# A fused graph layer and mixture of experts: VectorE's additions to node sums written one step behind their products, and a page's addition two steps behind

## The chip, the cores and the metric

The kernel runs on one core of one Trainium2 chip. Its engines are TensorE (PE: matrix products; PEld is its loading of weights), VectorE (DVE), ScalarE (ACT), GpSimd (POOL) and SyncE (SP). Each works through its own instruction stream in order; data passes between them through SBUF and, for products, through PSUM. The metric is the device time of one execution in microseconds (us).

## The reference, cut to what matters

There are 12,500 nodes with 256 features, and 212,500 weighted edges, sorted by destination. First a graph layer, then a mixture of experts with one expert a token:

```python
x = x + (segment_sum(layernorm(x)[src] * edge_weight[:, None], dst, 12500) @ W.T + b)
h = layernorm(x)                                     # tokens = nodes
probs = softmax(h @ gate_w + gate_b); idx = argmax(probs)      # 8 experts
# each expert takes at most C = 1954 tokens, in order
y = relu(h @ w1[idx] + b1[idx]) @ w2[idx] + b2[idx]            # 256 -> 1024 -> 256
x = x + nan_to_num(y * prob * kept)
```

The reference gathers a token over the limit from the last place of its expert and multiplies it by zero.

## The kernel before, in words

**Edges.** The 212,500 edges are cut into blocks of 128. For each block POOL gathers 128 rows of normalised features by an indirect DMA (`gather`, L708, into `m`). DVE builds a 128x128 mask `h` of destinations, scaled by edge weights (`onehot`, L731; L729 for self edges), and PE adds `h`-transposed times `m` into a sum `pw` of a group of 15 blocks, 1,920 edges (`product`, L742). When a group is done, ACT copies `pw` to SBUF as `ws` (L745; nine buffers). In the middle 88 groups, each group has 14 blocks of its own, and four groups share one further gather: 57 gathers for 4 groups. The blocks before round 112 are gathered from the raw input while a table of normalised features is written to HBM.

**The main loop.** After the table, everything is written by one Python loop with a counter (a *step* or *round* here). The order of instructions in each engine's stream is the order in which this loop writes them. In each round it writes, in this order: one gather (while there are any; the last is that of round 1594); an `own` load on SP at fixed rounds (L723); one of the `moves` (below; none in a round after a page's loads); one `put` of `pool_q` if there is one, or else one call of the generator that finishes the oldest computed page (`outs`); up to 8 masks ahead of need (`AHEAD`); one or two products, 16 gathers behind (`LEAD`); one call of each of a few start-up generators; one call of `nodes`; and one call of `experts`. A gather may not run more than 20 gathers ahead of the products (`LEASH`). A `yield` in a generator therefore means: what follows is written one round later.

**`nodes`** goes over the 98 tiles of 128 nodes, in chunks of 8 (the last chunks have 5, 4 and 1). For a tile it yields until the last group sum that the tile needs is there, and once more; writes the products that shift the group sums onto the tile (`pa`, L778), half by half with a yield after each; writes ACT's copy `aT` (L782) and the next tile's shift masks, and yields; writes two products with the weight matrix into `px` (L787), and then DVE's additions of `px` and the bias to the node's input, and its statistics (L790 and after). In PSUM, `pa`, `px` and other small products share the two buffers named `ms`. After a chunk comes `route`: gate, softmax, arg max and places; for the first ten chunks `sort` orders the chunk's tokens by expert and 64 `moves` (8 tiles x 8 experts) copy them to pages, one a round; for later chunks `put` scatters them through POOL. Then `listing` writes which pages of 128 tokens are full. `nodes` waits until the moves or puts have been written, and hands the listed pages on:

```python
                        while moves or pool_q:
                            yield
```

Up to chunk 9 pages are listed in pairs (33 pairs); from chunk 10 on singly (25 pages, of which the last 8 are the partly filled ones). `SLOTS` holds how many a chunk lists: (2, 4) for most, (1, 10) for chunk 10, then (1, 4) and (1, 3).

**`experts`** takes the pages one after another. SP loads a page and its expert's weights (L558 to L571, three buffers for weights and biases), up to two pages ahead; a page is started no sooner than 20 rounds after its loads (`LOADED`). Its product is a generator (`products`), called at paced rounds:

```python
PACE = {1: 2.3, 2: 3.0}
...
                    elif work and now[0] >= at:
                        at += PACE[got[0]]
```

The first layer is written in `ph` (L604) with ACT's relu into `hT` (L608), the second in `py` (L615; one buffer). Before a page's second layer, the next page is transposed (`turn`, L589). A single page takes its start and four calls, so 12 rounds; a pair takes its start and eight, 27 rounds.

**`finish`** ends a page, one part a call: DVE adds the bias to `py` (L625); ACT scales by the probability (L628); DVE clears non-finite values and adds the residual (L632 to L643, the last writes the row numbers `tok`); after three empty calls POOL scatters the rows to the output (L647, a *send*, one a call).

Of the kernel before, what the change touches and what calls it, by code (L numbers as in the profile page):

```python
# [122 lines left out]
def groups_of(t):  # L123
    return range(max(0, (P * PER * t - MARGIN) // GE),
                 min(NGR - 1, (P * PER * (t + 1) + MARGIN - 1) // GE) + 1)
# [12 lines left out]
def gnn_moe_kernel(ctx: ExitStack, tc: tile.TileContext, x, src, dst, ew, wT, gb, gate_w, gate_b,  # L138
# [85 lines left out]
    def ln_new(pool, n=CH):  # L224
        return pool.tile([P, n, 6], F32, name="bn"), pool.tile([P, n, 2], F32, name="mv")

    def ln_stats(ln, x_, j, rows):
        nc.vector.bn_stats(ln[0][:rows, j, :], x_)
        nc.vector.bn_aggr(ln[1][:rows, j, :], ln[0][:rows, j, :])
# [37 lines left out]
    class Ffn:  # L267
# [353 lines left out]
        def finish(self, of, pg, py, b2_sb):  # L621
            p4 = self.p4
            y = p4.tile([P, 2, D], F32, name="y", bufs=1)
            yv = y[:, :of, :]
            nc.vector.tensor_add(yv, py[:, :of, :], b2_sb[:, None, :].to_broadcast([P, of, D]))  # L625
            yield 1
            for a in range(of):
                nc.scalar.activation(y[:, a, :], y[:, a, :], AF.Copy, scale=pg[:, a, D + 2:D + 3])  # L628
            yield 1

            fin = p4.tile([P, 2, D], U8, name="fin")
            nc.vector.tensor_scalar(fin[:, :of, :], yv, 0.0, 0.0, op0=ALU.mult, op1=ALU.is_equal)  # L632
            hi = p4.tile([P, 2, D], F32, name="hi", bufs=1)
            nc.vector.tensor_scalar(hi[:, :of, :], yv, FLT_MAX, 1e4, op0=ALU.is_gt, op1=ALU.mult)
            z = p4.tile([P, 2, D], F32, name="z")
            zv = z[:, :of, :]
            nc.vector.tensor_scalar(zv, yv, -FLT_MAX, -1e4, op0=ALU.is_lt, op1=ALU.mult)
            yield 1
            nc.vector.tensor_add(zv, zv, hi[:, :of, :])
            nc.vector.copy_predicated(zv, fin[:, :of, :], yv)  # L640
            nc.vector.tensor_add(zv, zv, pg[:, :of, :D])
            to = p4.tile([P, 2, 1], I32, name="tok")
            nc.vector.tensor_copy(to[:, :of, :], pg[:, :of, D + 3:RW])  # L643

            def send(a):
                nc.gpsimd.nop()
                s = nc.gpsimd.indirect_dma_start(  # L647
                    out=out[:, :], out_offset=bass.IndirectOffsetOnAxis(ap=to[:, a, :], axis=0),
                    in_=z[:, a, :], in_offset=None, bounds_check=N - 1, oob_is_err=False)
                for o in self.sends:  # L650
                    tc.declare_no_dep(s.ins, o.ins, reason="each token is in one page")
                self.sends.append(s)

            for _ in range(3):
                yield 1
            for a in range(of):
                send(a)
                yield 1
# [20 lines left out]
    with tc.tile_pool(name="edges", bufs=1) as edges:  # L679
# [10 lines left out]
        with tc.tile_pool(name="p2", bufs=32) as p2, tc.tile_pool(name="p2h", bufs=12) as p2h, \  # L690
# [57 lines left out]
            def nodes():  # L748
                xs, shifts = [], {}

                def shift(t):

                    for g in groups_of(t) if t < NT else ():
                        s = p2o.tile([P, P], F32, name="s", bufs=8)
                        nc.vector.tensor_scalar(s, cols, float(P * t), win[:, g:g + 1], op0=ALU.add,
                                                op1=ALU.is_equal)
                        shifts[t, g] = s

                for c, (t0, nt, rows) in enumerate(CHUNKS):
                    rt = p3.tile([P, CH, RW], F32, name="rt")  # L760
                    ln = ln_new(p3)
                    for t in range(t0, t0 + nt):
                        for i in range(len(xs), min(t + 3, NT)):
                            x_ = p3.tile([P, D], F32, name="xt", bufs=4)
                            r = min(P, N - i * P)
                            nc.scalar.dma_start(x_[:r, :], x[i * P:i * P + r, :])
                            xs.append(x_)
                        if t == 0:
                            shift(t)
                        gs = groups_of(t)  # L770
                        while gs[-1] not in sums:
                            yield
                        yield
                        pa = ffn.psum("pa")[:, :2 * P]
                        aT = p2o.tile([P, 2 * P], F32, name="aT")
                        for k in range(2):
                            for g in gs:
                                nc.tensor.matmul(pa[:, k * P:(k + 1) * P],  # L778
                                                 sums[g][:, k * P:(k + 1) * P], shifts[t, g],
                                                 start=(g == gs[0]), stop=(g == gs[-1]))  # L780
                            yield
                        nc.scalar.copy(aT, pa)  # L782
                        shift(t + 1)
                        yield
                        px = ffn.psum("px")[:, :D]
                        for k in range(2):
                            nc.tensor.matmul(px[:rows, :], aT[:, k * P:k * P + rows], wT_sb[:, k, :],  # L787
                                             start=(k == 0), stop=(k == 1))
                        x1 = rt[:rows, t - t0, :D]
                        nc.vector.tensor_add(x1, xs[t][:rows, :], px[:rows, :])  # L790
                        nc.vector.tensor_add(x1, x1, gb_sb[:rows, :])
                        ln_stats(ln, x1, t - t0, rows)
                    yield from ffn.route(rt, ln, t0, nt, rows,
                                         by_expert[c % 3] if c < SORTED else None)
                    (moves if c < SORTED else pool_q).extend(ffn.put)
                    last = c == len(CHUNKS) - 1
                    if last:
                        nc.vector.scalar_tensor_tensor(n_bad, most, float(RUN), bad, op0=ALU.is_gt,
                                                       op1=ALU.add)
                    if last or SLOTS[c][1]:  # L800
                        if last:
                            lp = ffn.last()
                        yield from ffn.listing(*SLOTS[c] if not last else (1, LEFT, True))
                        li = ffn.li
                        while moves or pool_q:
                            yield
                        if last:
                            pages.extend((1, lp, 0, e) for e in range(E))
                        else:
                            of, n = SLOTS[c]  # L810
                            pages.extend((of, li, i) for i in range(n))
                        yield
# [320 lines left out]
            made = done  # L1133
            now, outs = [RAW], []
            a, b = nodes(), None
            extra = [ffn.fill(), check(), pack()]
            own_of = list(range(GR))
# [180 lines left out]
```

## Time and profile before

| | us |
|---|---|
| median of 10 runs | 2443.52 |
| lowest, highest | 2437.68, 2450.83 |
| profiled execution | 2447.49 |
| its span in the profile | 2445.6 |
| last gather (L708) starts | 2257.47 |
| last send (L647) starts | 2437.07 |

The profile is of one execution. For each engine it gives busy time and its share of the span; forty slices of the span, with the busy share in tenths; the idle time ahead of an instruction, with what released it; and, for a stretch, busy time and instructions of each engine (in brackets), the clock that TensorE was granted, the mean busy share of the DMA engines and GB/s. In a timeline a row holds the start, the duration, the engine, the line, the operation, output and inputs, the count, and in brackets the idle time ahead and its releaser. Line numbers are those of the kernel.

### The profile page before, as it was taken

To read this page: it belongs to the slowest core of one execution; us is meant where nothing else is said; L and a number is where in the kernel's file an instruction comes from. 1 tells how busy PE (TensorE), PEld (TensorE's weight loads), DVE (VectorE), ACT (ScalarE), POOL (GpSimd) and SP (SyncE) were. 2 spreads that over 40 slices of the span, in tenths; PEclk is the share of its full clock that TensorE was granted. 3 is DMA by queue.
4 is the path that set the end of the run, shared out by engine and by line. 5 is a ranking of instruction groups with operands and counts; after the bars stand their busy time and mean duration, and the time that the engine had idled before them with its cause. 6 is when DMAs were issued, how large, how long until landed. Compare 5 with 4: busy or idle time off the path is not lost. (4 is left out here: it accounts for less than half of the span.)

```text
span 2445.6 us, 34578 instructions
## 1 busy us (share of the span) xinstructions
PE 2017.9 (83%) x9483; PEld 1638.8 (67%) x9483; DVE 1337.8 (55%) x4667; ACT 537.1 (22%) x1405; POOL 1714.8 (70%) x1713
## 2 busy tenths in 40 slices
PE   2457657878698998998998998998988888889797
PEld 1346434555585786786876786777767767678686
DVE  7778985343354545654545545645545545545433
ACT  4760100010120221221311211211211211122333
POOL 7648887777667777777777777777777777777111
PEclk9678677778898999999999999999999999999999
DMA  8759444455746857767667668668668557487595
GB/s 291 240 183 336 135 130 136 125 156 161 246 131 170 300 161 213 245 171 248 196 184 244 205 173 263 188 169 276 185 167 289 149 161 234 145 285 257 180 296 192
DMA packets 301803, 502.50 MB, mean 205 GB/s; under 512 B 54349, under 2 KB 221864, under 8 KB 301593
## 3 DMA queue, kind: packets, MB, share of 16 engines
q0 software_dynamic: 81792, 221.87, 29.9%
q1 hardware_dynamic: 169890, 229.19, 29.8%
q10 hardware_dynamic: 49910, 49.06, 6.1%
q8 instruction: 81, 1.33, 0.2%
q14 instruction: 130, 1.06, 0.1%
HBM read 433.34 MB, written 110.76 MB: 222 GB/s over the span
## 5 line engine op out<-in xcount | busy, mean ns | idle before, releaser
L708 POOL DMA_INDIRECT m<-feat,src_i x1483 | 1497.2, 1010 | 485.2 <-issue 217.9
L742 PE MATMUL pw<-m,h 128*128 128x256 f32 x3322 | 1021.2, 427 | 275.4 <-DMA m<-feat,src_i 164.1
L742 PEld LDWEIGHTS pw<-m,h 128*128 128x128 f32 x3322 | 645.4, 210 | 489.3 <-DMA m<-feat,src_i 260.9
L731 DVE TENSOR_SCALAR h<-cols,rel,w_sb 128x128 f32<-128x128 f32 x1549 | 483.0, 364 | 352.8 <-PE pw L742 332.9
L604 PE MATMUL ph<-gT,w_sb 128*128 128x256 f32 (+1 forms) x1856 | 356.3, 342 | 2.7 <-ACT gT L592 2.7
L615 PE MATMUL py<-w_sb,hT 128*128 128x256 f32 x1456 | 349.9, 386 | 0.0
L604 PEld LDWEIGHTS ph<-gT,w_sb 128*128 128x128 f32 x1856 | 299.8, 195 | 32.7 <-ACT gT L592 3.1
L615 PEld LDWEIGHTS py<-w_sb,hT 128*128 128x128 f32 x1456 | 276.5, 194 | 36.2
L608 ACT ACTIVATE hT<-ph,b_sb 128x256 f32<-128x256 f32 (+1 forms) x464 | 168.0, 427 | 416.2 <-PE ph L604 365.0
L647 POOL DMA_INDIRECT out<-z,tok x91 | 91.1, 1001 | 165.2 <-DVE tok L643 113.4
L778 PEld LDWEIGHTS ms<-s,ws 128*128 128x128 f32 x1116 | 173.5, 213 | 25.1 <-ACT ws L745 8.1
L778 PE MATMUL ms<-s,ws 128*128 128x128 f32 x1116 | 173.6, 296 | 11.3 <-ACT ws L745 7.9
L790 DVE TENSOR_TENSOR rt<-xt,ms 128x256 f32<-128x256 f32 x98 | 41.2, 420 | 217.9 <-PE ms L787 216.9
L708 POOL DMA_INDIRECT m<-in_x,src_i x112 | 107.4, 959 | 53.5 <-issue 18.9
L745 ACT COPY ws<-pw 128x256 f32<-128x256 f32 x111 | 41.3, 372 | 434.6 <-PE pw L742 379.1
L625 DVE TENSOR_TENSOR y<-py,b_sb 128x512 f32<-128x512 f32 (+1 forms) x58 | 33.4, 576 | 187.2 <-PE py L615 187.1
L628 ACT ACTIVATE y<-y,pg 128x256 f32<-128x256 f32 x91 | 42.6, 503 | 345.0 <-DVE y L625 273.4
L787 PE MATMUL ms<-wT_sb,aT 128*128 128x256 f32 x392 | 106.9, 397 | 8.0 <-ACT aT L782 8.0
L782 ACT COPY aT<-ms 128x256 f32<-128x256 f32 x98 | 36.6, 373 | 290.3 <-PE ms L778 271.4
L787 PEld LDWEIGHTS ms<-wT_sb,aT 128*128 128x128 f32 x392 | 75.3, 197 | 25.0 <-ACT aT L782 14.7
L437 PE MATMUL ms<-rt,perm 128*128 128x260 f32 x160 | 55.1, 429 | 39.1 <-DVE perm L433 38.2
L333 PEld LDWEIGHTS ms<-gw_sb,xT 128*128 128x128 f32 x392 | 58.2, 206 | 36.7 <-ACT xT L328 34.6
(247 smaller groups left out, 1574.4 us busy)
## 6 DMA issues: line engine op xcount, KB each, us to landing
w_sb<-in_w SPq DMA_DIRECT2D x116, 1024.0 KB
buf<-by_expert SPq DMA_DIRECT2D x640, 65.0 KB
m<-feat,src_i POOLq DMA_INDIRECT x1483
buf<-fill SPq DMA_DIRECT2D x13, 1300.0 KB
xt<-in_x ACTq DMA_DIRECT2D x97, 128.0 KB
xt<-in_x SPq DMA_DIRECT2D x12, 1024.0 KB
feat<-xn ACTq DMA_DIRECT2D x12, 1024.0 KB
out<-rt ACTq DMA_DIRECT2D x11, 1024.0 KB
```

What stands on the lines that cost most here:

```text
L333: nc.tensor.matmul(pl[:rows, :], xT[:, k, :rows], gw_sb[:, k, :], start=(k == 0), stop=(k == 1))
L437: nc.tensor.matmul(ps, r[:rows, :], rt[:rows, j, :], start=True, stop=True)
L604: nc.tensor.matmul(ph[:, c:c + n], w1_sb[:, k, f * P:(f + 1) * P], xT[:, k * n:(k + 1) * n], start=(k == 0), stop=(k == 1))
L608: nc.scalar.activation(hT[:, f, :n], ph[:, c:c + n], AF.Relu, bias=b1_sb[:, f:f + 1])
L615: nc.tensor.matmul(py[:, a, :], hT[:, f, a * P:(a + 1) * P], w2_sb[:, f, :], start=(f == 0), stop=(f == F // P - 1))
L628: nc.scalar.activation(y[:, a, :], y[:, a, :], AF.Copy, scale=pg[:, a, D + 2:D + 3])
L647: s = nc.gpsimd.indirect_dma_start(out=out[:, :], out_offset=bass.IndirectOffsetOnAxis(ap=to[:, a, :], axis=0), in_=z[:, a, :], in_offset= ...
L708: i = nc.gpsimd.indirect_dma_start(out=m, out_offset=None, in_=x[:, :] if k < RAW else feat[:, :], in_offset=bass.IndirectOffsetOnAxis(ap= ...
L731: nc.vector.tensor_scalar(h, cols, rel[:, k:k + 1], w_sb[:, k:k + 1] if w is None else w, op0=ALU.is_equal, op1=ALU.mult)
L742: mms.append(nc.tensor.matmul(product.pw, hs.pop(i), m, start=first, stop=last))
L778: nc.tensor.matmul(pa[:, k * P:(k + 1) * P], sums[g][:, k * P:(k + 1) * P], shifts[t, g], start=(g == gs[0]), stop=(g == gs[-1]))
L787: nc.tensor.matmul(px[:rows, :], aT[:, k * P:k * P + rows], wT_sb[:, k, :], start=(k == 0), stop=(k == 1))
```

## The change

Two generators yield more often. In `finish`, two yields stand ahead of the addition of the bias to the page's second product, so that it, and all that follows in `finish`, is written two calls later. In `nodes`, one yield stands between a tile's products into `px` and the additions that read them, so that the additions, and all that follows in `nodes`, are written one round later. No instruction is added, removed or altered; their order in the streams is changed.

```diff
@@ finish
             p4 = self.p4
             y = p4.tile([P, 2, D], F32, name="y", bufs=1)
             yv = y[:, :of, :]
+            yield 1
+            yield 1
             nc.vector.tensor_add(yv, py[:, :of, :], b2_sb[:, None, :].to_broadcast([P, of, D]))
             yield 1
             for a in range(of):
@@ nodes
                         for k in range(2):
                             nc.tensor.matmul(px[:rows, :], aT[:, k * P:k * P + rows], wT_sb[:, k, :],
                                              start=(k == 0), stop=(k == 1))
+                        yield
                         x1 = rt[:rows, t - t0, :D]
                         nc.vector.tensor_add(x1, xs[t][:rows, :], px[:rows, :])
                         nc.vector.tensor_add(x1, x1, gb_sb[:rows, :])
```

## The prediction

> **What bounds the kernel now.** I read the page first, then the timeline of GpSimd (POOL), then busy times by stretch, the waits of TensorE (PE) and VectorE (DVE), and last the timeline of the end.
>
> ```profile
> PE 2017.9 (83%) x9483; PEld 1638.8 (67%) x9483; DVE 1337.8 (55%) x4667; ACT 537.1 (22%) x1405; POOL 1714.8 (70%) x1713
> PE   2457657878698998998998998998988888889797
> POOL 7648887777667777777777777777777777777111
> ```
>
> PE looks like the bound and POOL like an engine with 30% to spare. But POOL falls to 1 only in the last three slices (183 us). Its timeline says why it sits at 7 before that:
>
> ```profile
> 2246.05 0.95 POOL L708 DMA_INDIRECT m<-feat,src_i  x1 [0.30 <-issue]
> 2247.30 0.95 POOL L708 DMA_INDIRECT m<-feat,src_i  x1 [0.30 <-PE py L615]
> 2248.55 0.94 POOL L708 DMA_INDIRECT m<-feat,src_i  x1 [0.30 <-PE pw L742]
> 2249.80 1.07 POOL L647 DMA_INDIRECT out<-z,tok  x1 [0.30 <-DVE z L639]
> ```
>
> A gather of 0.95 us is followed by a fixed 0.30 us, whatever the trace puts down as releaser: a pitch of 1.25 us, and 1.29 for a send of a page (L647). By stretch:
>
> ```profile
> 1000.00:1500.00 500.00, 455.39 (x2181) 379.28 (x2180) 262.97 (x941) 98.20 (x233) 381.14 (x391) 0.97 0.67 204
> 1500.00:2000.00 500.00, 450.48 (x2172) 374.85 (x2171) 265.02 (x936) 100.98 (x238) 380.85 (x392) 0.98 0.67 207
> 2155.00:2257.50 102.50, 98.15 (x581) 87.09 (x581) 55.27 (x220) 27.09 (x80) 76.13 (x79) 0.97 0.77 259
> 2329.00:2445.60 116.60, 100.60 (x670) 92.35 (x669) 39.63 (x135) 41.40 (x135) 14.60 (x15) 0.95 0.79 254
> ```
>
> The columns are length, busy PE, PEld, DVE, ACT, POOL with counts, clock, DMA. 391 POOL operations and 391 gaps of 0.30 make 381.14 + 117.3 = 498 of 500 us: POOL has no pause there. PE follows it and catches up with it. In the stretch 1500 to 2240 its waits begin so:
>
> ```profile
> PE pw L742 <- DMA m<-feat,src_i: 40.4, 50, 3.2
> PE ms L437 <- DVE perm L433: 11.4, 4, 3.4
> ```
>
> Fifty times the gathered rows were not there yet. So up to the last gather (starts at 2257.5 us) POOL sets the time, one gather a step of the main loop. After it POOL is free and pages follow one another:
>
> ```profile
> 2390.81 3.62 PE L615 MATMUL py<-w_sb,hT 128*128 128x256 f32 x16
> 2394.27 3.73 PE L604 MATMUL ph<-gT,w_sb 128*128 128x128 f32 x32
> 2420.92 0.97 POOL L647 DMA_INDIRECT out<-z,tok  x1 [6.68 <-DVE tok L643]
> 2428.57 0.97 POOL L647 DMA_INDIRECT out<-z,tok  x1 [6.68 <-DVE tok L643]
> ```
>
> One page costs 7.65 us there (2428.57 − 2420.92), and PE fills it: 3.73 + 3.62 and two transposes. So a page computed beside the gathers costs POOL one send, 1.29 us, and a page left over costs 7.65 us. What counts is how many are left when the gathers end.
>
> **What the yields remove.** They add no instruction. Before, DVE stands at the additions:
>
> ```profile
> L790 DVE TENSOR_TENSOR rt<-xt,ms x98: 395/421/423, 197.2 to 2302.8; 128x256 f32<-128x256 f32 x97, 84x256 f32<-84x256 f32 x1
>   PE ms L787: 216.9, 86
> ```
>
> It stands 216.9 us at L790, and by the same view of L625 another 187.1 at the page's addition. From 704 us on, POOL shows one pause over 0.45 us before the last gather (2.85 at 2193), so none of this standing reaches POOL there; the AHEAD margin of masks covers it. I take 0. The bounds are a gain of all 15 us of POOL pauses between 600 and 704 us (they end with "PE pw"), and a loss of as much. After the last gather DVE's order is the same: a single page's addition moves from the step before the next page's start to the step after it, and nothing is written for DVE between. The two empty steps behind the last page hold no instruction: 0.
>
> The Trainium skill ("PSUM — Partial Sum Buffer", section "Engine vs sequencer instructions") says that VectorE's queue is strict FIFO, so all that stands behind a blocked addition waits too. By that rule alone the change would hand back up to 404 us of standing; by the rows above none of it is on the path.
>
> **What the yields cost: steps.** `nodes` is a chain of steps, one per round of the main loop. A chunk of 8 tiles needs 8 × 4 for the tiles, 28 in `route` and `sort`, 4 in `listing`, 60 more until its 64 moves are gone (one a round, 4 beside the listing), and 1: 125. The gathers supply a chunk in 8 × 128 × 17 / 1920 = 9.07 groups, at 57 steps for 4 groups: 129. So before, `nodes` has about 4 steps to spare and waits for sums. With one more step a tile it needs 133 and falls behind. Counting the rounds from the code: the list of chunk 1 comes at round 396 before and 397 after; then every 133, so that of chunk 9 at 397 + 8 × 133 = 1461, against 1440 as the gathers allow before. Chunk 10 takes 68 rounds instead of 63: 1529 against 1503, 26 late. (The same count puts 71 of 91 sends ahead of the last gather before; the trace has 71.)
>
> Chunk 10's list opens the 25 single pages, which then run on without a break, 12 rounds each (five calls paced 2.3 apart). The first starts at round 1552 instead of 1526; later lists, late by 1 to 8 rounds, find a backlog. The gathers still end at round 1594, as nothing slows them. So 26 / 12 = 2.17 pages fewer are done by then:
> - left over: 2.17 × 7.65 = +16.6 us;
> - sends that POOL no longer makes ahead of its last gather: a page is sent 17 rounds after its start before, 19 after, so 5 single pages before and 2 after: 3 × 1.29 = −3.9 us;
> - sum +12.7 us.
>
> Against this: from 2155 to 2257.5 PE idles only 4.35 us, so the deferred work might be no loss but only the same queue in another order. I count products against gathers: PE is 16 gathers behind at 2160 and 7 at 2260, about the 5 to 6 at which it waits for data. It has caught up when the gathers end. With the pages 26 rounds later it catches up sooner and then lacks data; the lag at the end can gain 1 or 2 rounds more (−2.5 us), or node work pushed later can leave it 4 behind (+5).
>
> **Other moves.** The page's addition frees its weights' bias buffer, for which SP's queue waits (138.5 us in 22 waits at L567); `own` loads queue behind that. The addition is written two steps (2.5 us) later; SP loads two pages ahead, so this is hidden, and if that cover failed, an `own` load would hold PE as it did in the trace at 5 to 16 us a time. The sends are POOL's and come two steps later, with DVE's `tok` long done. While `pool_q` drains, pages finish up to 8 rounds late, and one addition is then written a round ahead of the next product into `py`; a stall there is at most a step or two. `ws` has nine buffers: the sum of group 99 is written at round 1458, but group 90 is read for the last time at 1464, so ScalarE stands some 6 rounds (8 us) at that copy. Behind it stands a page's scaling, and no page product is written for PE in those rounds; cost 0, else up to 8.
>
> Against the profiled execution (2447.49 us, span 2445.6) the sum gives 2460.2, span 2458.3; that execution is 4 us over the median of the runs, 2443.52, from which 2456 follows.
>
> **Rivals.**
> - *PE is the bound, and is relieved (faster).* The 83% and the stretch before 2257.5 speak for it. Then left-over pages cost nothing, and PE's waits for DVE's `perm` (17.2 us from 600 to 1500, 11.4 from 1500 to 2240), which stands in DVE's queue behind the additions, come back: half of 28.6 is 14, so 2429 us. It decides if POOL's stretches show pauses, so that a faster PE brings gathers forward. The gapless rows of POOL speak against. 0.07.
> - *The slip is swallowed (same).* PE's queue is full to the end of the gathers anyway, and the late pages fill it as before: only 0 to 4 us, 2445. For it the 4.35 us of idle; against it the waits for gathered rows and the lag of 7. 0.08.
> - *The slip and a new wait (slower still).* ScalarE at the ninth `ws`, or `own` loads behind SP's later waits, stop the products by 8 to 15 us more: 2464 to 2471. It decides if POOL shows pauses ended by PE beyond 20 steps of lead. 0.12.
> - That the change does not what it says: not likely, each yield is one round for its generator.
>
> **How the numbers follow.** Forecast 0.73: 2456, with 2449 to 2463 as its own range (lag −2.5 to +5, runs' scatter about 4). About 0.2% (5 us) can be told from no change. Slower 0.73 + 0.12 = 0.85, same 0.08, faster 0.07. From 2446 to 2468 the range takes in the forecast and most of the third rival, and leaves out the first, most of the second and the edges.
>
> **What would show it.** Right: last gather near 2253 to 2254 us at the same 1.25 pitch; 68 sends ahead of it and 23 behind (20 now); the pitch of 7.65 unchanged; L790's standing smaller without effect; the first 128x128 product of `ph` later by some 30 us. Wrong: the last gather later by over 5 us (a new wait), fewer than two more sends behind it (no slip), or a last gather earlier than 2245 us (PE was the bound).

## The result and the profile after

| | before | after |
|---|---|---|
| median, us | 2442.98 (43 runs) | 2457.0 (12 runs) |
| ratio | 1 | 1.0057 [1.0047, 1.0067] |
| profiled execution, us | 2447.49 | 2451.36 |
| last gather starts | 2257.47 | 2244.00 |
| last send starts | 2437.07 | 2440.77 |
| sends ahead of the last gather | 71 | 68 |

The change costs 14.0 us (11.5 to 16.4). The page after, the same three rows:

```profile
PE 2032.5 (83%) x9483; PEld 1650.9 (67%) x9483; DVE 1336.7 (55%) x4667; ACT 535.1 (22%) x1405; POOL 1718.1 (70%) x1713
PE   2457667777987897997997997998998997989897
POOL 7648887777777777777777777777777777775111
```

The shares of busy time are those of before: nothing here tells that 14 us were lost. POOL's timeline around the last gather and at the end does (start, duration, then idle time ahead and its releaser):

```profile
2242.65 1.04 POOL L710 DMA_INDIRECT m<-feat,src_i  x1 [0.30 <-issue]
2244.00 0.94 POOL L710 DMA_INDIRECT m<-feat,src_i  x1 [0.30 <-DMA m<-feat,src_i]
2245.24 1.00 POOL L649 DMA_INDIRECT out<-z,tok  x1 [0.30 <-issue]
...
2424.62 0.97 POOL L649 DMA_INDIRECT out<-z,tok  x1 [6.68 <-DVE tok L645]
2432.27 0.97 POOL L649 DMA_INDIRECT out<-z,tok  x1 [6.68 <-DVE tok L645]
2440.77 0.97 POOL L649 DMA_INDIRECT out<-z,tok  x1 [7.53 <-issue]
```

Before the last gather the fixed 0.30 us is still there, and in the end a page still costs 7.65 us. But 23 sends now follow the last gather instead of 20, and the tail, which here is the time from the start of the last gather to the start of the last send, is 196.8 us instead of 179.6. More page work lies in it. The products of the first layer (`ph`) in the tail, before and after (stretch, length, PE, PEld, ACT with counts, clock, DMA share, GB/s):

```profile
2257.47:2437.07 179.60, 69.40 (x576) 68.33 (x576) 41.17 (x144) 0.97 0.72 232
2244.00:2440.77 196.77, 78.86 (x651) 77.81 (x649) 46.73 (x164) 0.96 0.75 246
```

A page has 32 of them, so 75 more are 2.3 pages. By stretch the gathers run as before, but for three pauses near 1590 us that hold POOL 3.2 us beyond its 0.30 (length, PE, PEld, DVE, ACT, POOL, clock, DMA share, GB/s):

```profile
1000.00:1500.00 500.00, 452.44 (x2157) 379.64 (x2155) 265.49 (x943) 96.39 (x228) 381.21 (x390) 0.96 0.66 199
1500.00:2000.00 500.00, 452.10 (x2144) 378.08 (x2145) 260.16 (x931) 98.58 (x233) 379.20 (x386) 0.95 0.68 208
```

VectorE's standing at the node addition, which the extra yield gives a later place in the stream, did not shrink (the line is L793 now):

```profile
L793 DVE TENSOR_TENSOR rt<-xt,ms x98: 405/422/423, 199.2 to 2291.4; 128x256 f32<-128x256 f32 x97, 84x256 f32<-84x256 f32 x1
  PE ms L789: 271.2, 88
```

### The profile page after: what moved, and what is told of

Same layout as the page of the kernel before. It is cut to its first block, busy times and chain, and to the rows that moved or that the text cites. A ratio compares the mean times of both kernels' runs of the same rounds, so it can differ in the third digit from the quotient of the medians.

```text
span 2449.6 us, 34558 instructions
## 1 busy us (share of the span) xinstructions
PE 2032.5 (83%) x9483; PEld 1650.9 (67%) x9483; DVE 1336.7 (55%) x4667; ACT 535.1 (22%) x1405; POOL 1718.1 (70%) x1713
## 5 line engine op out<-in xcount | busy, mean ns | idle before, releaser
L744 PE MATMUL pw<-m,h 128*128 128x256 f32 x3322 | 1041.2, 433 | 287.6 <-DMA m<-feat,src_i 181.0
L604 PE MATMUL ph<-gT,w_sb 128*128 128x256 f32 (+1 forms) x1856 | 350.4, 338 | 0.0
L793 DVE TENSOR_TENSOR rt<-xt,ms 128x256 f32<-128x256 f32 x98 | 41.2, 421 | 274.1 <-PE ms L789 271.2
L789 PE MATMUL ms<-wT_sb,aT 128*128 128x256 f32 x392 | 112.9, 415 | 15.4 <-ACT aT L784 15.4
L627 DVE TENSOR_TENSOR y<-py,b_sb 128x512 f32<-128x512 f32 (+1 forms) x58 | 33.1, 571 | 111.1 <-PE py L615 103.7
```

The lines of the kernel that those rows point to most:

```text
L604: nc.tensor.matmul(ph[:, c:c + n], w1_sb[:, k, f * P:(f + 1) * P], xT[:, k * n:(k + 1) * n], start=(k == 0), stop=(k == 1))
L744: mms.append(nc.tensor.matmul(product.pw, hs.pop(i), m, start=first, stop=last))
```

## Experiments

Times are medians beside those of before on the same chip. In e1 to e4 before took 2439.62 us, in e9 to e11 2440.42, in e12 2440.28. "The slip" is the prediction's main term: page lists that are handed on 26 rounds late, so that more pages are left when the gathers end. The chip of e5 to e8 ran before in 2912 us; only ratios within that group mean anything.

### The parts

**e1, the yield in `nodes` alone.**

```diff
             yv = y[:, :of, :]
-            yield 1
-            yield 1
             nc.vector.tensor_add(yv, py[:, :of, :], ...)
```

> Only the yield in nodes; finish as before. The theory of the slip (pages left over when the gathers end): the first single page starts at round 1552 instead of 1526 as with the whole change, 69 sends ahead of the last gather and 22 behind; +12 to +15 us against before, 2455 to 2458 us, so nearly all of the whole change's +14.0. Rival, that the page's addition two steps later carries part of the loss: less than +9. In the profile, the pauses of GpSimd between 630 and 705 us (15.0 us in the execution shown of before, none in that of the whole change) should be gone here if the nodes' yield removes them, and remain if the yields in finish do.

Measured: 2464.02 us, ratio 1.0089 [1.0072, 1.0106], +21.7 us by the ratio (24.4 by the medians): more than the whole change. The rounds came out as counted: 69 sends ahead of the last gather, tail 199.6 us. So the yield in `nodes` is enough for the whole loss, and the loss is larger than forecast. In its profile, which is the slowest of its six executions, the last gather stands at 2257.45, 13.5 us later than with the whole change; POOL's pauses beyond 0.30 us after round 112 explain most of that (15.8 us against 3.2). Why they go when the page's addition is also later was not settled.

**e2 and e10, the yields in `finish` alone** (and e8 on the slow chip).

```diff
                                              start=(k == 0), stop=(k == 1))
-                        yield
                         x1 = rt[:rows, t - t0, :D]
```

> Only the two yields in finish; nodes as before. The theory of the slip: all lists and page starts at the rounds of before (first single page 1526), 71 sends ahead of the last gather, so 0 within 3 us: 2440 to 2446. Rival, that the later page addition holds SP's queue or the next page's product: +3 to +10 us. Rival, that VectorE's freed time is worth something: VectorE's standing at the page's addition falls by about 80 us as with the whole change, and the time falls by 3 us or more.

> Only the yields in finish, a third time, because the first gave +8 (5 to 11) with no round of any page start moved, and a slower chip +0.2%. If the yields cost by themselves: +5 to +11 again. If it was scatter between executions: within 4 us of before.

> Only the yields in finish, once more. If the +8 us of the first time is the yields' doing, it comes again within 3 us, and the profile's tail (last gather to last send) is again about 182.0 us against 179.6 before; if it was scatter of the runs (two groups at 2444 to 2445 and 2449 to 2454), the time is within 4 us of before.

Measured: e2 2446.96 us, 1.0034 [1.002, 1.0047]; e10 2449.58 us, 1.0036 [1.0024, 1.0049]; e8 1.0023 [1.0003, 1.0043]. The cost of 7 to 9 us in e2 and e10 is clear of their intervals, though no page start moved and 71 sends stand ahead of the last gather in all of them. The profiles hardly show it: tails of 182.0 and 183.5 us against 179.6 and 181.5 in two profiles of before. One wait inside the tail grew, that of PE for DVE's `c` at L534, from 2.5 to 4.7 us. But e3 below, which has the same two yields and loses nothing, has a tail of 182.1 us and 4.8 us of this wait, so neither is the cost. The profiled executions were at or near the fast end of their sets (2444.47 and 2446.3). One number on record goes with the cost: the mean granted clock of the executions is 0.903 in e2 and e10, and 0.907 and 0.906 in those of before beside them (0.900 in e1, 0.906 in e3 and e4). Whether the lower clock costs the time or comes with it was not tried, so the cause is open. The two parts, +21.7 and about +8, do not add up to the whole +14.0.

### The slip without the additions, the additions without the slip

**e4, the slip alone.**

```diff
                         while moves or pool_q:
                             yield
+                        for _ in range(26 if c == 10 else 0):
+                            yield
```

> The kernel before, with no addition moved, but chunk 10 hands its list of pages on 26 rounds later (26 empty yields behind its puts), so that the first single page starts at round 1552 as with the change. The theory of the slip: 69 sends ahead of the last gather and the loss of the whole change, +11 to +14 us, 2454 to 2457. Rival, that the loss is made by the additions' order or by TensorE's queue being full anyway: 0 to +4, 2443 to 2447.

Measured: 2455.94 us, 1.007 [1.0056, 1.0085], +16.3 us by the medians (13.7 to 20.7 by the ratio), a little over the forecast. No addition is moved, and the whole loss is there. The timeline of POOL in e4 has the last gather at 2243.39 and 22 sends behind it, at the old pitch:

```profile
2243.39 0.95 POOL L708 DMA_INDIRECT m<-feat,src_i  x1 [0.30 <-issue]
...
2430.21 0.97 POOL L647 DMA_INDIRECT out<-z,tok  x1 [6.68 <-DVE tok L643]
2437.86 0.97 POOL L647 DMA_INDIRECT out<-z,tok  x1 [6.68 <-DVE tok L643]
2446.36 0.97 POOL L647 DMA_INDIRECT out<-z,tok  x1 [7.53 <-issue]
```

Its tail has 651 products of `ph`, as after the change:

```profile
2243.39:2446.36 202.97, 81.27 (x651) 80.22 (x649) 46.75 (x164) 0.93 0.71 234
```

Steps that hold no instruction cost 16 us, because the pages are handed on later and more of them are left when the gathers end. The fit is not exact: this tail is 21.5 to 23.4 us longer than the two of before, where the sum had 16.6.

**e3, the change with a tile's four rounds kept.**

```diff
                         while gs[-1] not in sums:
                             yield
-                        yield
                         pa = ffn.psum("pa")[:, :2 * P]
```

> The whole change, but one other yield of each tile (the one after the wait for the group sums) is taken out, so the additions still stand one round behind their products while a tile takes 4 rounds as before. The theory of the slip: lists at 1440 and 1503, first single page at 1526, 71 sends ahead of the last gather; the loss is gone, 2440 to 2447 us. Rival, that the additions' own lateness costs (a buffer of PSUM held a round longer, VectorE standing elsewhere): still +8 to +14, 2451 to 2457. A side cost is possible for both: the shifted products follow the copy of the last sum at once, so TensorE may stand for ScalarE's copy (7.9 us once before).

Measured: 2441.13 us, 1.0003 [0.9992, 1.0013]: the loss is gone. 71 sends ahead of the last gather (2252.66), the last send at 2434.75. One reserve: with four rounds a tile, the node additions stand in the round of before and it is their products that moved up. So e3 shows that distance between product and addition is free, not that later additions are. Its tail again has 576 products of `ph`. It also holds the two yields in `finish`, which alone cost 7 to 9 us; here they cost nothing that can be seen.

### Taking the slip away through the moves

**e9, the change with nine moves in eight rounds.**

```diff
-                n = MOVES if len(ffn.loads) == loads else 0
+                n = MOVES + (s % 8 == 0) if len(ffn.loads) == loads else 0
```

> The whole change, and in one round of eight two moves instead of one, so that a chunk's 64 moves take 57 rounds: nodes keeps pace with the gathers again, while the additions stay a round and two calls late (first single page at round 1527, 71 sends ahead of the last gather, 20 behind; in before 1526, 71 and 20). The theory of the slip: the loss is gone, within 4 us of before. Rival, that the lateness of the additions costs by itself: +8 us or more, as yields in finish alone did on the first chip.

Measured: 2471.75 us, 1.0129 [1.0107, 1.015], +31.3 us: a miss for the theory of the slip as forecast. The rival's "+8 us or more" holds as a number. The profile, which is of the slowest of the five executions (2480.42 us), shows where the time is: the slip is gone (71 sends ahead, 20 behind, tail 178.1 us), but the last gather starts at 2291.94. From 600 us to there POOL's pauses beyond 0.30 us come to 43.5 us, against 17.5 and 14.0 in the two profiles of before. PE's waits from 600 to 2240 us in e9 (total us, times, longest):

```profile
PE pw L744 <- DMA m<-feat,src_i: 90.5, 89, 5.0
PE pw L744 <- DMA own<-feat: 75.9, 10, 10.2
```

Before, in the same view:

```profile
PE pw L742 <- DMA m<-feat,src_i: 91.6, 121, 3.2
PE pw L742 <- DMA own<-feat: 21.9, 3, 15.7
```

The ten waits for `own` loads come one a chunk, about 178 us apart up to the eighth. SP's timeline in e9 shows one of them:

```profile
1141.37 0.40 SPq L558 DMA_DIRECT2D pg<-buf  x1
...
1145.01 0.48 SPq L558 DMA_DIRECT2D pg<-buf  x1
1145.69 4.38 SPq L565 DMA_DIRECT2D b_sb<-in_b  x1
...
1152.39 7.85 SPq L725 DMA_DIRECT2D own<-feat  x2
```

and PE's:

```profile
1165.94 1.22 PE L744 MATMUL pw<-own,h 128*128 128x256 f32 x2 [8.00 <-DMA own<-feat]
```

At the end of a chunk two pages' loads, ten DMAs, are written at once into SP's stream behind the last moves, and the `own` loads behind them come too late for PE. Before has this once:

```profile
632.96 1.22 PE L742 MATMUL pw<-own,h 128*128 128x256 f32 x2 [15.67 <-DMA own<-feat]
```

and POOL's pauses between 633 and 655 us follow at once. A chunk takes 128 rounds before, which is nine `own` loads at 14.25 rounds each, so every chunk meets them in the same place; with 133 rounds the place drifts and the waits are few and short (12.6 us in four after). In e9 the chunk is locked again, in a place where each chunk pays. The waits and their period are measured; that the locked place is the reason was not tried by itself, nor is it shown that the late additions have no part in the 31 us.

**e5 and e6, two moves a round** (`MOVES = 2`), with the change and with before, and **e7, the change again**, all on the slow chip.

> The whole change, with two moves written a round instead of one (MOVES = 2), so that a chunk's 64 moves take 32 rounds and nodes has spare rounds again: the additions stay a round and two calls late, the slip is gone (first single page at round 1527, 71 sends ahead of the last gather, 20 behind). The theory of the slip: within 3 us of before with two moves, and 2437 to 2447 us. Rival, that the additions' lateness itself costs (as yields in finish alone seemed to, +8): 5 to 10 us over before with two moves.

> The kernel before with two moves a round: pairs of pages are listed about 31 rounds earlier, but the single pages still start at round 1526, as chunk 10's last sums come when the gathers allow. The theory of the slip, by which only pages left over at the last gather count: 71 sends ahead of it, 0 within 4 us. Rival, that SP's queue is disturbed by moves in pairs and own loads come late: pauses of GpSimd ended by products, +5 us or more.

> The whole change once more, beside before on one chip, for the stretch 600 to 720 us: in the two profiles at hand GpSimd's pauses there are 15.0 us before and none after, and the last gather is 13.5 us earlier, of which the sum of the prediction has 3.9. If the change removes these pauses, none over 0.8 us is seen here again and the last gather is near 2244 to 2250 us; if they come and go between executions, some are seen. Time: +14 us against before as on the first chip (11 to 17).

Measured against before there: e5 1.0684 [1.065, 1.0718], e6 1.0799 [1.0772, 1.0827], e7 1.0079 [1.0051, 1.0107]. On that chip POOL did not set the pace (in e7 it pauses 146 us beyond its 0.30 after 2000 us, some 90 of them until PE and 42 until what the trace calls "remote"), so e5 and e6 do not answer their question. PE waits for `own` 183.9 us in 19 waits in e5 and 178.6 us in 19 in e6, against 52.4 in e7 and 54.4 in e8: the same kind of wait as in e9. e7 does repeat the slip: 68 sends ahead of the last gather and a tail of 217.2 us, against 71 and 198.6 in e8, 18.6 us more. Whether the early pauses come and go could not be read there.

### Two more

**e12, before once more.**

> The kernel before, unchanged, as a control, and for a second profile of it. Ratio 1.000 within 0.002; last gather to last send about 179.6 us again, pauses of GpSimd between 630 and 705 us again 10 to 15 us. If they are there, the whole change's profile without them shows something that the change does; if the last gather is then near 2250 us instead of 2257.5, the profiled execution of before that the prediction rests on was a late one in its first part. If the control differs by 0.3% from its twin, the +8 us of the yields in finish alone may be no more than that.

Measured: 1.0007 [0.9995, 1.002]. In its profile the last gather starts at 2251.55, the last send at 2433.02, so the tail is 181.5 us; the wait for `own` near 632 us is there again (18.37 us), and so are pauses of 12.3 us between 630 and 720. So this part of before is not chance. The last gather of the profile that the prediction rests on was some 6 us later than here. And before differs from itself by 0.07%, so the 7 to 9 us of e2 and e10 are more than the spread between two sets of one kernel.

**e11, pages earlier.**

```diff
-SLOTS = [(2, n) for n in (0, 3, 4, 4, 4, 4, 4, 4, 4, 2)] + [(1, n) for n in (10, 4, 3)]
+SLOTS = [(2, n) for n in (0, 3, 4, 4, 4, 4, 4, 4, 4)] + [(1, n) for n in (8, 6, 4, 3)]
-PACE = {1: 2.3, 2: 3.0}
+PACE = {1: 2.0, 2: 3.0}
```

> Before, turned the other way: chunk 9 lists 8 single pages in place of 2 pairs and chunk 10 lists 6 instead of 10, and a single page is called every 2.0 rounds instead of 2.3 (10.5 rounds a page). By the count of rounds the first single page starts at 1462, 74 sends stand ahead of the last gather and 17 behind, and 2.4 pages fewer are left over: by the sum of the prediction 2.4 x 7.65 = -18.4, and 3 x 1.29 = +3.9, so -14.5 us, if TensorE has the room (it idles 27 us from 2000 to 2155 us before, but only 4 us from 2155 to 2257). Rival, TensorE is full there: it holds the gathers through the leash of 20, pauses of GpSimd ended by products appear, and the gain is 0 to -6 us.

Measured: 2432.05 us, 0.9969 [0.9954, 0.9983]: 8.4 us faster than before, and faster than both kernels. 74 sends stand ahead of the last gather, at 2252.65, with no pause of POOL over 0.45 us from 720 us to there. So PE had the room, and the rule (a page left over costs its time after the gathers) works the other way too. The rest of the forecast gain was given back in the tail:

```profile
2404.35 0.97 POOL L647 DMA_INDIRECT out<-z,tok  x1 [7.69 <-DVE tok L643]
2413.02 0.97 POOL L647 DMA_INDIRECT out<-z,tok  x1 [7.70 <-DVE tok L643]
```

A page takes 8.67 us there, not 7.65. In the quicker order the next page is transposed behind `py` instead of ahead of it, and PE waits 1.1 us a page for ScalarE's copy `gT`.

## Why the prediction was right, and where it was not

**The bound** held: POOL's 1.25 us up to the last gather, 7.65 us a page behind it.

**The slip** is shown from both sides. Empty steps alone bring the loss (e4), and with the tile's four rounds kept the loss goes (e3). Its size was read from rounds: 68 sends ahead as counted, 2.3 pages of `ph` products more in the tail where the sum had 2.17 pages, and the tail grew by 17.2 us against one profile of before and 15.3 against the other, where the sum had 16.6. The first single page's product starts at 2166.74 us instead of 2141.64, 25 us later; the forecast was 30.

**The terms that were off.** The time came out at 2457.0 for 2456, but that close a hit is partly luck: the term for the last gather was off by 4 to 10 us one way, and a loss that the profiles do not show went the other.
- *"I take 0" for the start, with a gain of 15 us as bound.* The pauses did go: the wait of 15.67 us for an `own` load near 632 us and the pauses behind it are absent after, and the last gather is 7.5 to 13.5 us earlier where the sum had 3.9. Such a wait, of 14.6 to 18.4 us, is in every profile of the first chips with four rounds a tile (before, e12, e2, e3, e4, e10, e11). With five (after, e1, e9) none there is over 3.4 us, so the fifth round removes it. How much it gains is not settled, since e4 has the wait and 12.6 us of pauses behind it and its last gather stands at 2243.39 all the same. The prediction took the pauses as ended by PE. It knew that `own` loads had held PE for 5 to 16 us, but did not connect the two.
- *"A last gather earlier than 2245 us (PE was the bound)".* It came at 2244.00, and PE was not the bound. The mark was badly chosen, since it left out the gain that the sum itself had as a bound.
- *`finish` at nothing.* Alone it costs 7 to 9 us (e2, e10), and no profile shows where.
- *"SP loads two pages ahead, so this is hidden."* SP's waits for the page's addition at L567 grew from 138.5 us to 194.0 in e2, while PE's waits for `own` stayed near 20 us; that cover held there. With the whole change they fell to 92.5 us. What came late in e9 were `own` loads behind the pages' loads.
- *"L790's standing smaller".* It grew from 216.9 to 271.2 us, while that of the page's addition fell from 187.1 to 103.7. From 720 us to the last gather POOL's pauses beyond 0.30 us are 3.2 us after, so next to none of this reached it. By the strict FIFO order that the Trainium skill states ("PSUM — Partial Sum Buffer", section "Engine vs sequencer instructions"), whatever stands behind a blocked addition waits too. The trace agrees that VectorE stands there, and shows that it cost POOL next to nothing.
- *ScalarE "stands some 6 rounds (8 us)" at the ninth `ws`.* It did after the change, 10.8 us at group 99 (2033 us) and 11.0 at group 90 (1853 us). POOL has no pause over 0.45 us from 1600 us to the last gather, so the cost there is 0, as forecast.

The profiled execution after is 5.6 us under its median, that of before 4.5 over its own. From last send to last send the change costs 3.7 us by these two profiles, and 7.8 us against the profile of e12; what the other executions lose more is not seen in them and stays open. So does why `nodes` alone costs more than both together.

**The rivals.** PE as the bound is out: with more pages ahead of the last gather (e11) POOL does not pause. A slip that is swallowed is out by e4. The new wait behind SP did not come with the change (PE's waits for `own` fell from 21.9 to 12.6 us), but it exists: in e9 they are 75.9 us.

## What to carry to other kernels

Where a loop written by hand sets the order of all engines, count what an empty step does to the stage that ends last before counting what it hides: ask how many rounds the slowest chain has to spare, and what a piece of its work costs beside the bottleneck (1.29 us here) and after it (7.65 us). An engine that stands idle off the path, 404 us here, promises no gain until a row of the bottleneck shows that it waits for that engine. And a change of pace moves the places where transfers meet in a queue: loads that were just in time may be late in every turn, as in e9.

## What was not expected of the hardware

The same program took 2440 us on three chips and 2912 on a fourth; the tail there kept its 7.65 us a page, but the gather part stretched (last gather at 2707.7 us in e8 against 2252.3 in e2), with idle time of ACT, DVE and POOL put down to "remote" (242.6 us before DVE's masks in e8), which the profiles of the first chips do not show. The mean granted clock of those profiles is 0.847 in e8 and 0.904 in e2. What makes that chip slower was not tried.
